# A convolution layer's last stage: rows of e loaded ahead of the output store and the x load, and r3*x+k0 ahead of the copy of x on ScalarE

## The chip, the cores and the metric

The kernel runs on one core of a Trainium2 chip. A core has a matrix engine (TensorE, PE), three elementwise engines (VectorE or DVE, ScalarE or ACT, GpSimd or POOL), and SyncE (SP), which here issues nearly all transfers. Each engine takes its own instructions in order; engines wait for each other and for transfers through semaphores. A transfer is done by DMA engines, which all of SP's transfers share. The metric is the device time of the whole program in microseconds (us), and the figure compared is the median of several runs.

## The reference

Four layers are applied in turn to x of shape 1 x 256 x 256 x 128 (rows, columns, channels), each as `x = x + layer(gn(x))`, with gn a group normalization over the image: an attention layer, two triangle-multiplication layers, and a convolution layer. Only the last one matters here:

```python
t = relu(c1(x))                       # 3x3 convolution of 128 channels to one
y = concatenate([x[:, :1], x[:, 1:] + t[:, :-1]], axis=1)
u = relu(c1(y))
z_main = u + roll(y, 1, axis=1)       # the last two rows are special cases
...
v = relu(c2(z))                       # c2 is a 128x128 product per pixel (centre tap)
p = concatenate([z[:, :, :1], z[:, :, 1:] + v[:, :, :-1]], axis=2)
r = relu(c2(p))
q_main = r + roll(p, 1, axis=2)       # the last two columns are special cases
return q
```

t and u have one channel. So z is the normalized x, moved down one row, plus one number per pixel, which the kernel calls e (u plus the t that belongs there), added to all 128 channels.

## The kernel before

The four layers follow each other; the change lies in the last stage of the last layer (lines 1431 to 1711), which is written out by hand in the order in which each engine gets its instructions. Data stands with the 128 channels on the partitions. The image is cut into 32 groups of 8 rows (`R = 8`, `NR = 32`), each 128 x 2048 floats or 1 MB, and the one-channel images into 16 blocks of 16 rows (`NB = 16`), so two groups make one block. The normalization is folded in: r3 and k0 are a scale and an offset per channel.

For a group s:

- `load9` loads p_x (9 buffers), eight steps ahead.
- `taps`, six steps ahead, multiplies x by the nine taps' weights (PE, p_pp), adds an offset (ACT, p_st) and stores four small pieces to DRAM (sD).
- `load_block` gathers the nine shifted taps back as p_S. `sum_taps` adds them up (DVE, p_acc, L1494) and makes t (p_t, L1496 and L1497); `keep_t` stores t (tD), and `load_t` loads it back one row lower. `image_u` makes u from nine neighbours of t (L1511 to L1515), and `image_e` adds u and the loaded t to e (p_e, L1520) and stores it (eD).
- `load_e` loads the two groups' rows of e of a block as one partition's row each (p_er, 8 KB each), and `spread_e` copies such a row to all 128 partitions on POOL (p_eb, one buffer).
- `start_z` writes r3*x + k0 of a group to PSUM on ACT (p_zp, three or four instructions), and `finish_z` adds p_eb to it on DVE: p_z (L1566).
- `p_half` multiplies p_z by the centre tap (PE, p_pm) and makes p_pb from it (DVE, L1580). `q_half`, one step later, multiplies p_pb and makes p_q (DVE, L1594 and L1597). p_q begins as a copy of x with its offset (ACT, L1672), to which POOL adds p_pb (`residual`, L1586 to L1588).
- `emit`, two steps later, transposes p_q (PE, p_pt), copies it out of PSUM (ACT, p_o) and stores 1 MB of output.

PSUM has two pools: one of two buffers for p_pm, and one of two buffers that p_zp, p_pp and p_pt share in turn. The loop runs over steps s = 0 to 33. In the steady state an even step holds the sum of taps, t and u of a block, an odd step its e and the next gather of taps. SP's order over a pair of steps, from the end of an even one, is: output store, x load, load of t, store of e, four tap stores, two gathers p_S, output store, x load, two loads of e, store of t, four tap stores. A transfer that waits holds up all behind it. x loads end with step 23.

## Time and profile before

| | us |
|---|---|
| runs of the kernel before | 3385.05, 3386.2, 3391.52 (median 3386.2) |
| profiled execution, its run | 3389.84 |
| span in the profile | 3388.1 |
| last stage, from the first x load (2951.2) to the end of the span | 437 |
| PE busy in the whole span | 3085.6 (91%) |
| DVE busy | 2281.1 (67%) |
| ACT busy | 2030.0 (60%) |
| POOL busy | 1666.1 (49%) |

The shares are averages over four layers with different limits. For this change only the last stage counts, and in it the order of time: a row of the profile gives the start and the duration of an instruction, its engine, its line, what it writes and reads, and in brackets how long the engine had been idle before it and what ended that. "SPq" rows are the issue of a transfer, not the transfer itself.

### The profile page before, as it was taken

How to read it: one execution, taken by the hardware profiler on the slowest of the kernel's cores; microseconds unless marked ns; L12 is line 12 of the kernel's file. 1: busy time of each engine (PE TensorE's matmuls, PEld its weight loads, DVE VectorE, ACT ScalarE, POOL GpSimd, SP SyncE). 2: the span in 40 equal slices, each digit the busy share in tenths (PEclk: the TensorE clock that was granted, in tenths of full speed). 3: DMA queues.
4: the chain of work that ended last, by engine and by line, in shares of the span. 5: the costliest groups of instructions: out<-in, count | busy, mean ns of one | idle time of the engine just before them, and what ended most of it. 6: DMA issues, size and time to landing. Idle time of an engine off the chain costs nothing. (4 is left out here: it accounts for less than half of the span.)

```text
span 3388.1 us, 52060 instructions
## 1 busy us (share of the span) xinstructions
PE 3085.6 (91%) x20018; PEld 1636.1 (48%) x20018; DVE 2281.1 (67%) x2612; ACT 2030.0 (60%) x2241; POOL 1666.1 (49%) x908
## 2 busy tenths in 40 slices
PE   5669999999999999967996999999999999748888
PEld 4415555555555555533432444445999333214444
DVE  5627888888888888853555445454555777648787
ACT  3567777777777777734686445443444566636665
POOL 4055777777777777720483000001555344436565
PEclk8889999999999999989897999999999999879999
DMA  9982333333333333369597668676999899736764
GB/s 367 365 310 85 108 121 108 120 108 120 108 120 108 120 108 120 108 270 346 195 409 302 256 257 312 230 258 251 353 349 347 308 334 335 286 115 198 215 191 131
DMA packets 298104, 749.49 MB, mean 221 GB/s; under 512 B 74713, under 2 KB 145323, under 8 KB 248699
## 3 DMA queue, kind: packets, MB, share of 16 engines
q1 hardware_dynamic: 289787, 735.24, 60.6%
q0 software_dynamic: 7776, 9.81, 0.8%
q8 instruction: 160, 2.62, 0.3%
q10 hardware_dynamic: 288, 1.05, 0.1%
q14 instruction: 93, 0.76, 0.1%
HBM read 458.35 MB, written 287.64 MB: 220 GB/s over the span
## 5 line engine op out<-in xcount | busy, mean ns | idle before, releaser
L564 DVE TENSOR_TENSOR p_e<-p_S,triT 128x1024 f32<-128x1024 f32 x512 | 609.4, 1212 | 144.3 <-PE p_S L554 144.3
L574 POOL TENSOR_TENSOR p_es<-p_e 128x1024 f32<-128x1024 f32 x256 | 602.8, 2366 | 124.4 <-issue 65.5
L572 ACT ACTIVATE p_e<-p_e,mbT 128x1024 f32<-128x1024 f32 x512 | 552.0, 1138 | 59.8 <-DVE p_e L564 59.7
L1167 PE MATMUL p_pm<-p_zn,wf 128*128 128x512 f32 x1040 | 449.3, 593 | 2.1 <-ACT p_a L1202 1.9
L539 PE MATMUL p_mm<-p_xn,w 128*128 128x512 f32 x768 | 406.6, 613 | 0.3 <-DVE p_v L534 0.3
L1167 PEld LDWEIGHTS p_pm<-p_zn,wf 128*128 128x128 f32 x1040 | 196.5, 190 | 254.9 <-issue 246.3
L554 PE MATMUL p_S<-p_q,p_k 32*128 32x256 f32 x4096 | 295.7, 401 | 3.3 <-DVE p_e L564 3.3
L554 PEld LDWEIGHTS p_S<-p_q,p_k 32*128 32x128 f32 x4096 | 186.1, 184 | 159.2 <-PE p_mm L530 91.7
L513 POOL TENSOR_TENSOR p_xn<-p_xn,p_rs 128x1024 f32<-128x1024 f32 x63 | 151.2, 2401 | 207.7 <-ACT p_xn L508 131.6
L1852 PE MATMUL tp_z<-p_B,tp_at 128*128 128x256 f32 x1024 | 250.6, 388 | 0.8 <-DMA p_B<-bD 0.5
L1239 POOL DMA_DIRECT2D rs__17906<-rs2D x4 | 2.0, 514 | 506.9 <-DVE p_zn L1160 506.9
L587 PE MATMUL p_o<-p_e,p_v 128*32 128x256 f32 x4096 | 247.6, 382 | 0.0
L1282 POOL TENSOR_TENSOR k<-k,p_sq 128x512 f32<-128x512 f32 x128 | 163.0, 1273 | 156.9 <-ACT p_sq L1280 156.9
L1392 POOL TENSOR_TENSOR p_x<-p_x,p_g 128x2048 f32<-128x2048 f32 x30 | 136.3, 4543 | 160.5 <-DVE p_g L1379 97.2
L1852 PEld LDWEIGHTS tp_z<-p_B,tp_at 128*128 128x128 f32 x1024 | 185.2, 191 | 23.6 <-DVE tp_at L1843 1.6
L1586 POOL TENSOR_TENSOR p_q<-p_q,p_pb 128x2024 f32<-128x2024 f32 x32 | 144.9, 4529 | 70.0 <-DVE p_pb L1580 69.5
L539 PEld LDWEIGHTS p_mm<-p_xn,w 128*128 128x128 f32 x768 | 126.5, 191 | 105.5 <-issue 89.5
L1281 DVE TENSOR_TENSOR k<-tp_z,k 128x512 f32<-128x512 f32 x128 | 88.5, 692 | 127.2 <-ACT p_sq L1280 127.2
L587 PEld LDWEIGHTS p_o<-p_e,p_v 128*32 128x32 f32 x4096 | 120.0, 109 | 109.3 <-ACT p_g L545 41.5
L1278 ACT COPY p_K<-tp_z 128x512 f32<-128x512 f32 x128 | 74.9, 585 | 157.8 <-PE tp_z L1852 157.8
L545 ACT ACTIVATE p_g<-p_mm,bgh 128x512 f32<-128x512 f32 x128 | 87.9, 687 | 131.4 <-PE p_mm L539 131.4
L530 PEld LDWEIGHTS p_mm<-w,p_xn 128*128 128x128 f32 x1024 | 134.4, 191 | 61.1 <-issue 60.6
(377 smaller groups left out, 5945.9 us busy)
## 6 DMA issues: line engine op xcount, KB each, us to landing
p_x<-x2T SPq DMA_DIRECT2D x60, 1024.0 KB
x<-x1T SPq DMA_DIRECT2D x51, 1024.0 KB
p_x<-in_x_dram SPq DMA_DIRECT2D x32, 1024.0 KB
p_x<-xT SPq DMA_DIRECT2D x64, 512.0 KB
x2T<-x SPq DMA_DIRECT2D x32, 1024.0 KB
aD<-p_a SPq DMA_DIRECT2D x32, 1024.0 KB
bD<-p_b SPq DMA_DIRECT2D x32, 1024.0 KB
p_A<-aD SPq DMA_DIRECT2D x32, 1024.0 KB
```

Of the source, the lines that this page charges most:

```text
L513: nc.gpsimd.tensor_tensor(xn, xn, groups[g]["rs"], ALU.mult)
L539: nc.tensor.matmul(pm, lhsT=w, rhs=t["xn"][:, cs_], start=True, stop=True)
L554: nc.tensor.matmul(Ss[h // 2][:, h % 2, u, :], lhsT=t["k"][hp, r * N + u * P : r * N + (u + 1) * P], rhs=t["q"][hp, r * N : (r + 1) * N], ...
L564: nc.vector.tensor_tensor(e[:, :, 2 * p : 2 * p + 2, :].rearrange("p u h n -> p h u n"), Ss[p], triT[:, 2 * p : 2 * p + 2, :, :], ALU.add,)
L572: nc.scalar.activation(e[:, u, :, :], e[:, u, :, :], AF.Exp, bias=mbT[:, u, i : i + 1])
L574: nc.gpsimd.tensor_tensor(es, e[:, 0, :, :], e[:, 1, :, :], ALU.add)
L587: nc.tensor.matmul(t["o"][hp, r % 2, :], lhsT=t["v"][:, r * 2 + u, hp], rhs=e[:, u, h, :], start=(u == 0), stop=(u == 1),)
L1167: nc.tensor.matmul(pm[:, c, :], lhsT=wf2[:, i, :], rhs=zns[s][:, k * CK : (k + 1) * CK], start=True, stop=True)
L1282: nc.gpsimd.tensor_tensor(k2, k2, sq, ALU.add)
L1392: nc.gpsimd.tensor_tensor(xs7[s], xs7[s], gts[s], ALU.add)
L1586: nc.gpsimd.tensor_tensor(q[:, :, 1 : N - 2], q[:, :, 1 : N - 2], pb[:, :, 0 : N - 3], ALU.add)
L1852: nc.tensor.matmul(pz[:, t, :], lhsT=at[:, u, t * P : (t + 1) * P], rhs=Bc[:, u, :], start=(u == 0), stop=(u == 1))
```

## The change

In a step, `start_z` of the next group is called before the copy of x to p_q instead of after it. `load_e`, which an even step called near its beginning (after the x load and after the output store of the step before), is called at the end of the odd step before it, after `load_block` and ahead of `emit`. The same blocks are loaded, and no buffer, shape or operation differs.

```diff
             if s % 2 == 1 and 2 < b < NB:
                 load_t(b)
-            if s % 2 == 0 and 3 < b <= NB:
-                load_e(b - 1)
             if s < NR:
                 pbs[s] = sb.tile([P, R, N], F32, name="p9_pb")
                 nc.scalar.activation(pbs[s][:, :, 0:1], zs[s][:, :, 0:1], AF.Identity, bias=kcol[:, 0:1])
+                if s + 1 < NR:
+                    start_z(s + 1)
                 qs[s] = sb.tile([P, R, N], F32, name="p9_q", bufs=3)
                 nc.scalar.activation(qs[s], xs[s], AF.Identity, bias=kcol[:, 2:3])
-                if s + 1 < NR:
-                    start_z(s + 1)
                 p_half(s, 0)
                 p_half(s, 1)
                 del xs[s]
...
                 taps(xs[s + LEAD], (s + LEAD) * R, 4)
             if s > 1 and s % 2 == 1 and b + 1 < NB:
                 load_block(b + 1)
+            if s > 1 and s % 2 == 1 and b < NB:
+                load_e(b)
             if s > 1:
                 emit(s - 2)
```

## The prediction

> **What bounds the kernel now.** The edit touches only the last layer, so I read the page for its extent (the last 437 us of a 3388.1 us span), then the chain of waits there, then the list of waits, then the order of time through one pair of steps. The steps come in pairs, because a block of 16 rows is two groups of 8. The waits, from 2990 us on (who waited, for whom, us in total, times, longest):

> ```profile
> POOL p_eb L1543 <- DMA p_er<-eD: 58.5, 9, 17.3
> DVE p_z L1566 <- POOL p_eb L1543: 30.3, 10, 4.2
> DVE p_e L1520 <- DMA p_t<-tD: 20.7, 11, 9.8
> DVE p_z L1566 <- ACT p_zp L1551: 0.2, 1, 0.2
> SPq L1611 <- DMA p_x<-x3T: 18.9, 10, 2.8
> ```

> Both row transfers (e and t) are late in every pair, and p_z never waits for ScalarE's p_zp. One pair in order of time (start, duration, engine, line):

> ```profile
> 3197.81 0.32 SPq L1522 DMA_DIRECT2D eD<-p_e  x1
> ...
> 3200.82 1.05 SPq L1474 DMA_DIRECT2D p_S<-sD  x2
> ...
> 3201.97 0.99 SPq L1611 DMA_DIRECT2D out_dram<-p_o  x1
> ...
> 3203.05 3.75 SPq L1449 DMA_DIRECT2D p_x<-x3T  x1
> ...
> 3206.85 1.30 SPq L1535 DMA_DIRECT2D p_er<-eD  x2
> ...
> 3211.80 2.29 POOL L1543 PARTITION_BROADCAST p_eb<-p_er  x1 [6.58 <-ACT p_q L1687]
> 3211.82 0.41 SPq L1611 DMA_DIRECT2D out_dram<-p_o  x1
> ...
> 3214.12 2.36 DVE L1566 TENSOR_TENSOR p_z<-p_zp,p_eb 128x1024 f32<-128x1024 f32 x2 [3.41 <-POOL p_eb L1543]
> ...
> 3220.33 1.03 DVE L1520 TENSOR_TENSOR p_e<-p_u,p_t 128x33 f32<-128x33 f32 x1 [1.22 <-DMA p_t<-tD]
> ...
> 3221.38 0.32 SPq L1522 DMA_DIRECT2D eD<-p_e  x1
> ```

> The e rows are issued 9.04 us after the store of e, behind the tap rows p_S, 1 MB of output and 1 MB of x, and the chain has 4.76 us from issue to landing (3211.61). The broadcast p_eb had been free to start since 3205.2 (end of POOL's p_q), so it is 6.6 us late; p_z then loses 3.41 us. After it POOL runs p_q (3214.18) and the next p_eb (3219.15 to 3221.45), and p_e ends with that: er landing plus 9.8 us. The t rows land some 1.1 us before. From the e store at 3056.92 to that at 3291.81 are ten pairs: 23.49 us a pair. PE has 9.77 us of work a step (3054.88 to 3064.65 between two p_z products, nothing waiting), DVE about 10 us, so a pair could take some 20.

> [...] er has 4.8 to 6.8 us to landing behind those two megabytes, 2.0 us with an empty queue. [...] this pair, after the x loads are over, has a p_eb that is hardly late:

> ```profile
> 3302.28 2.29 POOL L1543 PARTITION_BROADCAST p_eb<-p_er  x1 [3.07 <-DMA p_er<-eD]
> 3302.32 2.28 DVE L1515 TENSOR_SCALAR p_u<-p_u,b 128x33 f32<-128x33 f32 x1
> ...
> 3305.71 5.30 PE L1572 MATMUL p_pm<-p_pb,w2c 128*128 128x512 f32 x8 [2.65 <-DVE p_pb L1580]
> ...
> 3310.93 1.06 PE L1455 MATMUL p_pp<-p_x,w1f 128*32 128x512 f32 x8
> ...
> 3314.87 0.32 ACT L1670 ACTIVATE p_pb<-p_z,kcol 128x8 f32<-128x8 f32 x1
> ```

> L1515 took 2.28 us instead of 0.24 and ends with p_eb. [...] Here 8 products took 5.30 us after 2.65 us of idle, 3.70 elsewhere; gaps of 2.65, 2.87 and 3.29 us were all followed by slow work, gaps up to 1.88 us never, 2.12 partly, 2.35 not.

> **The change, part by part.** Nothing is added or removed; each engine has the same instructions, and the order changes on ACT and SP alone.

> (1) Both e transfers (8 KB each; 0.6 us of issue when nothing backs up) move ahead of one output store and one x load, and ahead of nothing else. They come after p_S, so their wait for the e store's landing (1.44 us) is over. They should land about 0.5 us after p_S: some 7.5 us after the e store instead of 13.8. The output store and x load follow about 1.3 us later in issue, hidden by the p_S transfers still draining (x is loaded two steps before its use). Reaching further: the program gives SP's transfers eight semaphores in turn, so each waits for the one eight places earlier. Before, the odd step's output store waits for the x load (3211.82, the L1611 row above); now it waits for er, and the next x load for an output store long landed. So t is no longer held by that.

> (2) p_zp (2.67 us) goes ahead of the copy of x to p_q (2.00 us) on ACT. p_z didn't wait for p_zp: worth 0 there. The copy is 2.67 us later, and POOL's p_q needs it. In the slow pair above p_pb starts on ACT 3.94 us after p_pp on PE; the copy ended 2.2 us later, at p_pp + 6.15, and now ends at + 8.82. VectorE ends p_pb at + 7.73 (3318.66). So POOL is held 1.0 us (from p_pb's end + 0.17 to + 1.2), in even steps; in odd ones p_pb comes later than the copy.

> (3) What is late next. POOL's p_q to p_eb is 4.97 us (3214.18 to 3219.15). p_eb then starts at p_pp + 8.82 + 0.10 + 4.97 = 13.89, and L1496 (two SBUF inputs) comes at + 7.73 + 6.25 = 13.98: the whole 2.29 us of p_eb fall on VectorE. Before, POOL sat waiting for er there, and L1496 ran free. The cover was er's lateness, and part 1 takes it away.

> The new loop, from the odd step's p_pb on VectorE to the next odd one: first half to PE 1.33, products 3.70, p_pp to ACT's p_pb 3.94, ACT 4.88 (0.21 + 2.67 + 2.00), hand-over 0.10, POOL 4.97, p_eb 2.29, rest of the image work on VectorE 1.64 (3206.61 to 3208.25): 22.85 us. PE meanwhile: p_z products start at p_pp + 2.81, one step of 9.77, products 3.60: idle from p_pp + 16.18 to + 19.15, 2.97 us. Such gaps were slow in 3 of 3; [...] Price 5.30 - 3.70 = 1.60, so 1.28: 24.13 us a pair, against 23.49.

> Sum: the first pair still gains (copy ends 3060.9, p_eb 3065.97 to 3068.26, p_pb 3069.9, then 2.46 + 0.17 + 4.97 + 2.29: e store at 3079.85 for 3080.47), -0.6. Nine pairs, 9 x 0.64 = +5.8. The two pairs without x loads (3291.81 to 3337.91, 46.1): 24.13 + 23.1 (the last has no p_pp, 1.0 less), +1.1. First steps: their p_q waits hide behind DMA. Last steps: PE-bound at 8.8 us each, POOL 7.3, 0. Together +6.3. The profiled span of 3388.1 (its run 3389.84) becomes 3394.4; the median of the runs lies 1.9 under that span, so **3392 us**, 0.17% more: within the 0.2% that a measurement of this kernel can tell from no change.

> Is t in time? tD follows L1496, at the e store + 11.6 (13.2 behind a slow clock); then p_st's four stores (1.4) and the output store, at about + 13.3 (14.9), where it is + 14.0 before; from there to t's landing 8.4 us as before: 21.7 (23.3), or 22.7 if the x load lands 0.4 late and gates it. The pair takes 22.85 (24.45): 0.15 to 1.15 us to spare.

> **Rivals.** *Slower, from the clock.* Every gap drops the clock: 24.45 a pair, 9 x 0.96 - 0.6 + (24.45 + 23.45 - 46.1 = 1.8) = +9.8: 3396. For it: 3 of 3 gaps, and a slow loop has the same 2.97 us gap. Against: [...] 2.35 us was free. It decides above 85% of the gaps; with half of them the sum is about +1.

> *Faster, e's gain kept.* If the copy is not late (ScalarE further ahead than in the pair I took), p_eb starts 1.0 us sooner and blocks L1496 for 1.2 instead of 2.2; the gap shrinks to about 2 us, the clock holds, and t sets the pair at 22.2: 10 x -1.29 - 1.5 = -14: 3372. For it: 30.3 us of p_z's waits and 18.9 of the store's go. Against: ACT's 3.94 us from p_pp holds in every step that I looked at. It decides where POOL's p_q starts within 0.3 us of p_pb.

> *t takes e's place.* If x and output still hold t for 22 to 23 us and p_e follows, pairs stay at 23.5: 3386. It would need p_q to be in time and t late.

> **How the numbers follow.** Loop with part of the gaps slow, within 0.2%: 0.37, and t in e's place 0.06: same 0.43. Clock slow nearly always, or more delay than I count: slower 0.40. Gain kept: faster 0.17. Range 3374 to 3399: from near the fast rival to the slow one plus 3 us for output and x pushed back by er. The likeliest's own is 3385 to 3393.

> **What would show it.** POOL's wait for p_er gone from the steps with x loads, p_z's wait for p_eb near 0, SP's wait of L1611 for p_x gone. L1496 at some 2.4 us instead of 0.26 in most even steps, POOL's p_q released by ACT's p_q instead of p_pb, PE gaps near 3 us with half-speed clock after most. Pairs of 24.1 us. Wrong if L1496 stays short, if p_q follows p_pb at once, or if p_e waits over 2 us for p_t.

## The result and the profile after

| | kernel before | changed kernel |
|---|---|---|
| first comparison, median of the runs | 3391.52 us (13 runs) | 3400.83 us (13 runs) |
| their ratio, 95% interval | | 1.0043 [1.0022, 1.0063] |
| second comparison, median of the runs | 3389.58 us (38 runs) | 3404.12 us (21 runs) |
| their ratio, 95% interval | | 1.0032 [1.0015, 1.0050] |
| profiled execution, its span | 3388.1 us | 3396.0 us, and 3416.9 us in a second one |
| fourth store of e (the prediction's first, 3056.92 before) to the end | 331.2 us | 340.75 us, and 340.97 us in the second one |
| a pair of steps, mean of the ten after that store | 23.49 us | 24.23 us, and 24.24 us in the second one |

The change makes the kernel slower, by 0.3 to 0.4%. (The ratios are not those of the medians, which are 1.0027 and 1.0043; the first is that of the means.) The forecast was 3392 us, and the measured 3400.8 lies 1.8 us above its range. The last two rows say it more sharply than the medians: single runs of either kernel spread over some 30 us, and where the two profiles of the changed kernel show such a spread (21 us), it had all come up by the start of the last layer, 17 us of it in the stage just before, which the change doesn't touch. From the fourth store of e to the end, the two agree within 0.3 us.

The waits of the changed kernel from 2990 us on (who waited, for whom, us in total, times, longest):

```profile
POOL p_q L1586 <- DVE p_z L1566: 73.3, 14, 7.1
...
PE p_pm L1572 <- DVE p_pb L1580: 42.5, 14, 5.3
...
DVE p_e L1520 <- DMA p_t<-tD: 18.7, 9, 9.5
...
POOL p_eb L1543 <- DMA p_er<-eD: 16.9, 1, 16.9
...
POOL p_q L1586 <- ACT p_q L1672: 7.2, 2, 5.4
```

The broadcast's wait for e has gone from 9 times to one (in the layer's first steps). p_z's wait for p_eb (30.3 us before) and the output store's wait for x (18.9 us) are in the list no more. In their place PE waits 42.5 us for VectorE's p_pb, which has to be done before PE can have a PSUM buffer back; it waited 22.7 us for that before. In the first row the profile names p_z as what released POOL's p_q; the pair below shows that the copy of x on ACT ended last.

A pair in order of time (start, duration, engine, line; in brackets the idle time before and what ended it):

```profile
3199.04 0.32 SPq L1522 DMA_DIRECT2D eD<-p_e  x1
...
3202.73 1.99 ACT L1672 ACTIVATE p_q<-p_x,kcol 128x2048 f32<-128x2048 f32 x1
3203.21 1.36 SPq L1535 DMA_DIRECT2D p_er<-eD  x2
...
3204.85 4.52 POOL L1586 TENSOR_TENSOR p_q<-p_q,p_pb 128x2024 f32<-128x2024 f32 x1 [5.74 <-DVE p_z L1566]
...
3209.82 2.22 DVE L1496 SCALAR_TENSOR_TENSOR p_t<-p_acc,b,p_in 128x41 f32<-128x41 f32 x1
...
3209.83 2.29 POOL L1543 PARTITION_BROADCAST p_eb<-p_er  x1
...
3213.68 2.46 DVE L1580 SCALAR_TENSOR_TENSOR p_pb<-p_pm,kcol,p_z 128x1020 f32<-128x1020 f32 x2
...
3215.01 5.34 PE L1572 MATMUL p_pm<-p_pb,w2c 128*128 128x512 f32 x8 [2.93 <-DVE p_pb L1580]
...
3222.71 0.77 DVE L1520 TENSOR_TENSOR p_e<-p_u,p_t 128x33 f32<-128x33 f32 x1 [0.91 <-DMA p_t<-tD]
...
3223.51 0.32 SPq L1522 DMA_DIRECT2D eD<-p_e  x1
```

Read from the top. The e rows are issued 4.17 us after the store of e, where it was 9.04, and the first lands 2.82 us after its issue, where it took 4.76 (1 MB of output and 1 MB of x ahead of it). p_pb ended at 3203.64 and the copy of x at 3204.72: POOL's p_q starts right after the copy. So p_eb falls on the same moment as L1496 on VectorE, which takes 2.22 us instead of 0.26 and ends with p_eb (at 3212.04 and 3212.12). p_pb is late, PE stands for 2.93 us, and the next eight products take 5.34 us instead of 3.70. That repeats: L1496 takes 2.08 to 2.23 us in every pair from 3064 us on. The trace also records the clock granted to PE, here 1.0 or 0.5 of full speed. The gap of the first pair, as long as the others (2.94 us at 3069.5), was followed by full speed; from the gap at 3092.1 on each has a stretch of half clock, 11 of them between 3092.0 and 3337.8, and two of these, at 3139.8 and 3262.7, last 6.83 us instead of 3.41. The first pair took 22.76 us, the second 22.81 (its p_e waits 1.7 us for t, so that the slow products show only in the next). The eight after it took 24.59 us on average; the two with a long stretch took 25.81 and 25.60.

The table by stretches shows the clock: us from the span's start, length, busy time of PE, PE's weight loads, DVE, ACT and POOL with the number of instructions, granted clock, DMA share, GB/s. First the kernel before, then the changed one:

```profile
3060.00:3300.00 240.00, 209.65 (x831) 100.01 (x831) 194.14 (x247) 153.62 (x185) 148.13 (x83) 0.99 0.69 203
```

```profile
3060.00:3300.00 240.00, 211.32 (x792) 99.92 (x792) 200.65 (x238) 147.22 (x177) 142.45 (x80) 0.92 0.67 198
```

PE is busier in the changed kernel and shows 39 matmuls fewer in the same 240 us: 0.92 of the clock instead of 0.99.

### The profile page after: what moved, and what is told of

Its sections match the earlier page's. It is cut to its first block, busy times and chain, and to the rows that moved or that the text cites. A ratio compares the mean times of both kernels' runs of the same rounds, so it can differ in the third digit from the quotient of the medians.

```text
span 3396.0 us, 52049 instructions
## 1 busy us (share of the span) xinstructions
PE 3096.8 (91%) x20018; PEld 1640.9 (48%) x20018; DVE 2297.5 (68%) x2612; ACT 2029.9 (60%) x2241; POOL 1666.8 (49%) x908
## 3 DMA queue, kind: packets, MB, share of 16 engines
q10 hardware_dynamic: 288, 1.05, 0.1%
## 5 line engine op out<-in xcount | busy, mean ns | idle before, releaser
L1572 PE MATMUL p_pm<-p_pb,w2c 128*128 128x512 f32 x256 | 139.8, 697 | 42.5 <-DVE p_pb L1580 42.5
```

Source lines behind the costliest of these rows:

```text
L1572: nc.tensor.matmul(pm[:, 2 * c : 2 * c + 2, :], lhsT=w2c, rhs=src[:, r : r + 2, :], start=True, stop=True)
```

## The experiments

Two measures are used throughout: "the layer" below is the time from the fourth store of e to the end in the profiled execution (331.2 us before, 340.75 changed), and "a pair" is the mean of the ten pairs after that store. Ratios are to the kernel before, with a 95% interval.

**Each half of the change alone.** First the move of `load_e`, without that of `start_z`:

```diff
-            if s % 2 == 0 and 3 < b <= NB:
-                load_e(b - 1)
...
+            if s > 1 and s % 2 == 1 and b < NB:
+                load_e(b)
             if s > 1:
                 emit(s - 2)
```

> The kernel before with the move of load_e alone; start_z stays behind the copy of x. My theory (late copy -> p_eb meets L1496 whole -> PE gap of 2.9 us -> half clock): with the copy in time POOL's p_q follows p_pb, p_eb runs from p_pp + 12.87 to + 15.16 and holds L1496 for 1.2 us instead of 2.2; the PE gap shrinks to about 2 us, the clock holds in most pairs, and the pair is 21.8 by the loop or 22.2 by t: 12 to 16 us under the kernel before. Rival (the early e alone costs: any meeting of p_eb and L1496, or the output store and x load behind e, slows the pair): pairs of 23.5 us or more, no gain or a loss.

Measured: 3380.77 us against 3392.22, 0.9958 [0.9941, 0.9974]; the layer 317.1 us (14.1 less), a pair 22.59 us. Three rows of its order of time, from two pairs:

```profile
3162.41 5.40 PE L1572 MATMUL p_pm<-p_pb,w2c 128*128 128x512 f32 x8 [1.90 <-DVE p_pb L1580]
...
3181.75 0.93 DVE L1496 SCALAR_TENSOR_TENSOR p_t<-p_acc,b,p_in 128x41 f32<-128x41 f32 x1
...
3185.65 3.70 PE L1572 MATMUL p_pm<-p_pb,w2c 128*128 128x512 f32 x8 [1.75 <-DVE p_pb L1580]
```

L1496 is held for about 1 us (0.86 to 1.25 in all) instead of 2.2, the PE gap is 1.3 to 2.1 us instead of 2.9, and only three of them dropped the clock. VectorE's wait for t has grown to 24.1 us from 3060 to 3300 us (9.2 in the changed kernel); that t limits the pair here is shown further below. This is what the rival *Faster, e's gain kept* in the prediction describes, and its sum of -14 us. A meeting of p_eb with L1496 that holds it for 1 us, and not for 2, does not make the kernel slower.

Then the move of `start_z` alone:

```diff
+                if s + 1 < NR:
+                    start_z(s + 1)
                 qs[s] = sb.tile([P, R, N], F32, name="p9_q", bufs=3)
                 nc.scalar.activation(qs[s], xs[s], AF.Identity, bias=kcol[:, 2:3])
-                if s + 1 < NR:
-                    start_z(s + 1)
```

> The kernel before with the move of start_z alone; load_e stays behind the output store and the x load. My theory: er lands 6.6 us later than POOL could use it, so a copy of x that is 2.67 us later (p_q held 1.0 us) is hidden, L1496 stays at 0.26 us, and the time is that of before within 3 us. Rival (the late copy is what costs in the changed kernel, by itself): 5 to 10 us slower, with POOL's p_q held by the copy and long PE gaps.

Measured: 3391.16 us, 0.9992 [0.9978, 1.0006]; the layer 329.3 us, a pair 23.53. Its waits between 3060 and 3300 us, and two rows of a pair:

```profile
POOL p_eb L1543 <- DMA p_er<-eD: 34.5, 6, 6.7
...
DVE p_z L1566 <- POOL p_eb L1543: 30.3, 10, 4.2
...
POOL p_q L1586 <- ACT p_q L1674: 29.8, 9, 4.6
```

```profile
3201.12 4.53 POOL L1586 TENSOR_TENSOR p_q<-p_q,p_pb 128x2024 f32<-128x2024 f32 x1 [3.23 <-ACT p_q L1674]
...
3206.38 0.26 DVE L1496 SCALAR_TENSOR_TENSOR p_t<-p_acc,b,p_in 128x41 f32<-128x41 f32 x1
```

POOL's p_q now follows the copy of x, so the copy is late here too; but e is later still, p_eb comes after L1496, and nothing is lost. The two halves alone give -14.1 and -1.9 us in the layer, together +9.6: all of the loss is in their meeting.

**The clock.** In the changed kernel the second half of the p_z product is done twice, into the same PSUM tile, in odd steps (1.8 us of PE work in the 2.9 us gap; 16 steps, 29 us of work added in all):

```diff
         def p_half(s, h):
             rows_ = slice(h * H, (h + 1) * H)
             pm = product9(zs[s], h)
+            if h == 1 and s % 2 == 1:
+                for c in range(2):
+                    r = h * H + 2 * c
+                    nc.tensor.matmul(
+                        pm[:, 2 * c : 2 * c + 2, :], lhsT=w2c, rhs=zs[s][:, r : r + 2, :], start=True, stop=True
+                    )
```

> The changed kernel with the second half of the p_z product done twice, into the same PSUM tile, in each odd step: 1.8 us of PE work put into the 2.8 to 2.9 us gap, nothing else moved. If the clock is what makes pairs of 24.2 to 25.8 us: no half clock in these gaps, the loop's own 22.85 us a pair, 11 pairs x 1.6 to 1.8 us = 17 to 20 us under the changed kernel, some 3380 us or 7 to 10 us under the kernel before. If the lock and POOL's chain alone make the pair and the clock is hidden: no change against the changed kernel, 0.4% above before; if PE is the bound: slower by up to 29 us.

Measured: 3392.62 us, 0.9993 [0.9975, 1.0010]; the layer 325.2 us, which is 15.5 under the changed kernel, a pair 22.67. The same stretch of the table, and the gap in one pair:

```profile
3060.00:3300.00 240.00, 227.49 (x885) 107.78 (x884) 214.23 (x257) 158.18 (x189) 152.44 (x85) 1.00 0.70 208
```

```profile
3179.91 1.88 PE L1583 MATMUL p_pm<-p_z,w2c 128*128 128x512 f32 x4
...
3182.89 3.70 PE L1572 MATMUL p_pm<-p_pb,w2c 128*128 128x512 f32 x8 [1.10 <-DVE p_pb L1586]
```

More work on the busiest engine made the layer shorter. The gap is 1.10 us, no stretch of half clock is left in the ten pairs (one follows at 3320.3, and one over the last 6 us, as at the end of every kernel here), L1496 still takes 2.06 to 2.25 us in all pairs but one (1.56), and the pair is the loop's own. So of the changed kernel's pair of 24.2 the clock is 1.6 us. The expectation had 17 to 20 us under the changed kernel, a little more than the 15.5 found. The time of the whole program can't tell this kernel from the kernel before: by the layer it would be 6 us, or 0.18%, shorter, which lies within the interval.

The same addition on the kernel with `load_e` moved alone:

> The kernel with load_e moved alone, with the second half of the p_z product done twice in odd steps: the 1.9 us gaps are nearly filled. If the clock costs that kernel only where a gap dropped it (3 of 10 pairs x 1.6 us): no half clock, 4 to 6 us under it, pairs of 22 us limited by t. If filled PE time pushes t or q: no gain.

Measured: 3375.86 us, 0.9960 [0.9945, 0.9975]; the layer 313.2 us (3.9 under that kernel), a pair 21.82, clock 1.00. By the trace it is near what was expected (4 to 6 us, no half clock); the ratios of the two (0.9958 and 0.9960) cannot tell them apart.

**The changed kernel once more**, unchanged:

> The changed kernel again, unchanged, beside the others on one chip. If the slow clock in every pair is all there is, its last layer is the loop of the first profile: pairs of 24.2 to 24.6 us, 10 us over the kernel before (ratio near 1.003); if the 14.6 us of the first comparison hold (ratio near 1.0043), part of the loss is still without a cause.

Measured: 3404.12 us against 3389.58, 1.0032 [1.0015, 1.0050]; the layer 340.97 us, with the same pairs to within 0.1 us and the same two long stretches of half clock. The loss in the layer, 9.6 to 9.8 us, is 0.28 to 0.29% and lies within both intervals.

**The meeting of p_eb and L1496.** It can be taken away without leaving work out: p_eb is put behind an operation on POOL that waits for VectorE's work on u. The first attempt moved the scalar operation on u to POOL:

```diff
-            nc.vector.tensor_scalar(k["u"], k["u"], b1, 0.0, ALU.add, ALU.max)
+            (nc.gpsimd if b > 2 else nc.vector).tensor_scalar(k["u"], k["u"], b1, 0.0, ALU.add, ALU.max)
...
                 residual(s)
-                spread_e(s + 2)
+                late = s > 1 and s % 2 == 0 and b < NB
+                if not late:
+                    spread_e(s + 2)
...
                     image_u(b)
+                    spread_e(s + 2)
```

> The changed kernel with the last operation on u (L1515, scalar add and max) done on POOL, and the even step's p_eb behind it, so that p_eb starts after VectorE's image work (p_t, p_prod, p_u) instead of beside it; same instructions otherwise. If the meeting of p_eb and L1496 opens the PE gap: L1496 back at 0.26 us in even steps, the gap near 1 us, no half clock there, and the pair 22.85 - 2.0 = 20.9 us by the loop, or some 22 by t: 15 to 25 us under the kernel before. If the late copy of x is what counts: the gap and the pairs of 24 us stay.

Measured: 3665.4 us, 1.0797 [1.0765, 1.0828]. POOL's rows in one pair:

```profile
3307.44 2.30 POOL L1543 PARTITION_BROADCAST p_eb<-p_er  x1 [8.14 <-issue]
3316.87 4.49 POOL L1586 TENSOR_TENSOR p_q<-p_q,p_pb 128x2024 f32<-128x2024 f32 x1 [7.12 <-ACT p_o L1610]
...
3327.72 2.30 POOL L1543 PARTITION_BROADCAST p_eb<-p_er  x1 [5.99 <-issue]
3337.03 4.62 POOL L1586 TENSOR_TENSOR p_q<-p_q,p_pb 128x2024 f32<-128x2024 f32 x1 [7.01 <-issue]
```

POOL stands idle for 6 to 9 us ahead of nearly every broadcast and every p_q, and a pair takes 43.2 us. L1496 is 0.26 us, but with such gaps the run says nothing on the changed kernel's clock. The trace has what precedes them, instructions that no other run has in the last stage (number; shortest, median and longest in ns; first and last start):

```profile
L1543 POOLq MODIFY_POOL_CONFIG  x56: 1/1/24, 3040.3 to 3617.3; - x56
L1586 POOLq MODIFY_POOL_CONFIG  x56: 129/129/129, 3050.1 to 3625.1; - x56
```

Two of them stand ahead of each of 28 broadcasts and 28 p_q, and from the second one to the work behind it 5.5 to 8.9 us pass. So the idle time came with the scalar operation in POOL's work, at each change between the broadcast and the additions, and each time behind these instructions; what POOL does in these 6 to 9 us no row shows.

The second attempt keeps to kinds that POOL had there already: the two-operand addition on u goes to POOL, p_eb behind it, and the scalar operation stays on VectorE and moves to `image_e`, a step later.

```diff
         def image_u(b):
...
-            nc.vector.tensor_tensor(k["u"], k["u"], k["acc"][:, 0:BW], ALU.add)
-            nc.vector.tensor_scalar(k["u"], k["u"], b1, 0.0, ALU.add, ALU.max)
+            (nc.gpsimd if b > 2 else nc.vector).tensor_tensor(k["u"], k["u"], k["acc"][:, 0:BW], ALU.add)
...
         def image_e(b):
             k = blocks.pop(b)
             e = sb.tile([P, BW], F32, name="p9_e")
+            nc.vector.tensor_scalar(k["u"], k["u"], b1, 0.0, ALU.add, ALU.max)
```

with `spread_e` moved as above.

> The changed kernel with the even step's addition on u (L1514, two operands) done on POOL, p_eb behind it there, and the scalar add and max on u moved from image_u to the start of image_e, a step later: the same instructions otherwise, and on POOL only kinds that stand there already. If the meeting of p_eb and L1496 opens the PE gap: L1496 at 0.26 us, the gap at 1 us or less, no half clock there, the loop at 22.85 - 2.0 - 0.4 = 20.5 us, t (whose store follows L1496 2 us earlier) at some 21 to 22: 15 to 25 us under the kernel before. If the late copy of x is what counts, the gap and the pairs of 24 us stay.

Measured: 3376.47 us, 0.9961 [0.9941, 0.9980]; the layer 310.7 us, 30 under the changed kernel and 20.5 under the kernel before, a pair 22.12. One pair:

```profile
3188.25 0.26 DVE L1496 SCALAR_TENSOR_TENSOR p_t<-p_acc,b,p_in 128x41 f32<-128x41 f32 x1
...
3189.81 0.26 POOL L1514 TENSOR_TENSOR p_u<-p_u,p_acc 128x33 f32<-128x33 f32 x1 [3.19 <-DVE p_u L1513]
3190.04 2.29 POOL L1543 PARTITION_BROADCAST p_eb<-p_er  x1
3190.97 3.70 PE L1572 MATMUL p_pm<-p_pb,w2c 128*128 128x512 f32 x8 [0.53 <-DVE p_pb L1580]
```

L1496 is short in every pair and the gap that it opened is 0.53 us here and no longer in the others, although p_zp still goes ahead of the copy of x. Two stretches of half clock are left, where none was expected; they follow gaps of 2.32 and 2.54 us in the other step of a pair, not at the place of L1496. So the late copy costs through this meeting alone, which the next run confirms. But the pair is 22.1 us and not 20.5: VectorE now waits 30.7 us for t in ten pairs. The same on the kernel with `load_e` moved alone:

> The same rearrangement of u and p_eb on the kernel that moves load_e alone. If the remaining 1.1 us of L1496 and the 1.9 us PE gaps are what hold that kernel's pair at 22.6: pairs of 21 to 22 us, limited by t. If t already sets the pair there (VectorE waited 1.5 us for it), nothing more than the earlier tD store, 1 us a pair, is gained.

Measured: 3373.85 us, 0.9951 [0.9929, 0.9973]; the layer 311.7 us, a pair 22.16. With the copy early or late it is the same pair. And t holds the pair already with `load_e` moved alone: VectorE's wait for it is 31.1 us here, and the earlier store of t brings 0.4 us a pair, where up to 1 was expected.

**What sets the pair then.** In the odd step the load of t goes ahead of the x load:

```diff
-            load9(s + 8)
             b = s // 2 + 2
             if s % 2 == 1 and 2 < b < NB:
                 load_t(b)
+            load9(s + 8)
```

> As the last one, and the odd step's load of t ahead of that step's x load. If t behind 1 MB of x sets the pair: VectorE's wait for p_t before p_e goes, the e store comes 1 to 2 us earlier, and pairs fall to PE's 20 to 21 us: 20 to 30 us under the kernel before. If the tD store or the semaphore that t shares with earlier transfers sets it: no change from the run without this move.

Measured: 3357.68 us, 0.9904 [0.9878, 0.9931]; the layer 294.0 us, a pair 20.36. VectorE's wait for t between 3060 and 3300 us, first in the kernel without this move, then with it:

```profile
DVE p_e L1520 <- DMA p_t<-tD: 31.1, 10, 4.1
```

```profile
DVE p_e L1520 <- DMA p_t<-tD: 2.2, 4, 1.0
```

No PE gap over 0.8 us and no half clock is left up to 3280 us, and PE is busy for 215.6 of the 220 us from 3060 us on: PE is the bound. The same with p_zp ahead of the copy, as in the changed kernel:

> The last rearrangement (e early, u and p_eb deferred, t ahead of the x load) with p_zp ahead of the copy of x as in the changed kernel. If the order of p_zp and the copy matters only through the meeting of p_eb with L1496: PE-bound pairs of 20.2 to 20.5 us as without it, within 3 us of that run. If the later copy has a price of its own (POOL's p_q 1.0 us later, p_eb and p_z after it): pairs of 21 us or more, 8 us or more above it.

Measured: 3350.49 us, 0.9869 [0.9842, 0.9896]; the layer 294.5 us, a pair 20.29. The order of p_zp and the copy, which cost the changed kernel some 24 us against `load_e` moved alone (340.75 to 317.1), is worth nothing here. Both versions are faster than the kernel before, by 1.0 and 1.3%, and so than the changed one; they were run six and four times, on different chips, and their intervals overlap.

## Why the prediction was wrong

*Right: the order of events.* The forecast put p_eb at p_pp + 13.89, L1496 at + 13.98, and PE's idle time from + 16.18 to + 19.15. In the pair above (p_pp at 3195.91) they are at + 13.92, + 13.91, and + 16.17 to + 19.10. POOL's p_q is held 1.0 us by the copy, as said. The loop without the clock, 22.85 us by the sum, is 22.76 in the first pair and 22.67 with the gap filled.

*Right: the parts by themselves.* Part 2 "worth 0" while e is late: the run with it alone shows -1.9 us in the layer and no difference in the times. Part 1's gain of 14 us, in the rival that keeps it: 14.1. Only their meeting costs, as part 3 said. The rival *t takes e's place* didn't come about here, but t is what limits the pair as soon as the meeting is gone.

*Right in effect, not in size.* t was to have 0.15 to 1.15 us to spare. VectorE does wait for it, 0.91 us in the pair shown and 1.7 at most, 9.2 us in 8 of the ten pairs; that is under the 2 us that the prediction names as a sign of being wrong, and it doesn't set the pair: with the gap filled the wait is 19.2 us and the pair 22.67. The prediction shows L1515 held beside p_eb (2.28 us instead of 0.24) and says of L1496 that it has two SBUF inputs. L1515 has one tensor, p_u, and a value per partition, b, so it is no example of two tensors. L1496, with the two tensors p_acc and p_in, and L1520, with p_u and p_t, show the same in the profiles before and after: from 3040 us on, the 15 of L1496 and the 25 of L1520 that ran beside a p_eb ended 0.08 to 0.09 us before it, L1496 after 1.04 to 2.23 us (0.26 alone), L1520 after 0.33 to 1.81 (0.20 at the shortest). p_eb took 2.29 to 2.30 us each time. L1580 and L1594, which read a PSUM tile, kept their 1.27 to 1.28 us beside it, and L1494, with one tensor, its 1.34 to 1.36. Why L1515 was held, in its one meeting there, isn't shown.

*Wrong: the share of slow gaps.* This is the step that failed in the account of the change. The sum's 1.28 us a pair are 0.8 of the price of 1.60; the 0.8 was the author's estimate, and it was too low. From the second pair on every gap was slow, and two drops lasted twice as long: 24.59 us a pair where the sum had 24.13. The two pairs without x loads were slow as well, 48.7 us where the sum had 47.2. Together the layer is 9.6 us longer (9.8 in the second profile) where the forecast had 6.3. That is the rival *Slower, from the clock*, worked out at +9.8 us and 24.45 a pair. I gave it and other delays 0.40 and the partly slow loop 0.37.

| window | PE idle in it, us | windows | the next one at half clock |
|---|---|---|---|
| at full clock | 1.88 to 2.87 | 27 | 27 |
| at full clock | 0 to 1.83 | 718 | 0 |
| at half clock | 0.67 to 1.53 | 5 | 5 |
| at half clock | 0 to 0.56 | 27 | 0 |

In these windows the border is some 1.85 us of idle time inside one, and, to stay slow, some 0.6. It is a border of this stage: over their whole spans the profiles before and after have 74 drops to half clock, 11 of them behind a window with 0.99 to 1.83 us of idle time, and six windows with 1.85 to 1.96 us had none behind them; 13 windows at half clock with under 0.6 us were followed by another. In the stage it sorts all the gaps: the 1.88, 1.90 and 2.09 us gaps with `load_e` moved alone lay each within one window, the other one of 1.88 and that of 1.89 were divided by a border, and the forecast's "gaps up to 1.88 us never" was a matter of place. By this border a gap of 2.94 us is free only if a border divides it into two parts under 1.85, that is, if the gap ends 1.09 to 1.85 us after a border: (1.85 - 1.09) / 3.41 = 0.22 of all places. For a place drawn at random, then, some 0.78 of the gaps would be slow, near the 0.8 of the sum; that is an estimate from the table.

But the place is not random in a loop. Against the window's border nearest to it, the first eleven gaps of the changed kernel end at + 1.3 us (the first pair, free), then + 0.1, + 0.6, + 0.7, - 0.9, - 0.4, + 0.1, + 0.4, + 0.7, - 1.0, - 0.4: a pair of 24.2 to 24.5 is a little over seven windows (23.9), so the place moves on by some 0.4 us a pair; at + 0.7 the half-clock window holds over 0.6 us of the gap, the drop lasts a second window, and the longer pair (25.6 to 25.8, seven and a half windows) throws the place back to about - 1. It never comes to the free places from + 1.1 on. The second profile of the changed kernel shows the same sequence. The borders of 1.85 and 0.6 are read from the traces, and only the runs with the gap filled test them by an edit (1.1 to 1.2 us of idle time, no drop); no run moved the window.

*Wrong too, and more in us: the base.* The forecast started from the 3386.2 us of three runs. The same kernel has 3391.5 us in 13 runs, these three among them, and 3389.6 to 3392.2 in later series. So of the 8.8 us between forecast and result some 5 are the base, and 3.3 the clock's share. The range of 3374 to 3399 had room for the slow rival on the low base, and none for a base that three runs had put 5 us too low.

## What to carry to other kernels

Two edits that each cost nothing or gain can lose together: the early e was cover for the late copy, so before removing a wait, ask what has been running beside something slow only because of that wait. The 2 us that L1496 lost beside p_eb reached PE as a gap of 2.8 to 2.9 us, and the half clock behind it added 1.6 us a pair (24.2 against 22.67 with the gap filled). Here a PE gap of 2 to 3 us was free or slow by how much of it fell into one window, and in a loop that lasts nearly whole windows that can be slow in almost every turn, as here (11 of 12). And a single median of three runs was 5 us off for a change of 10. The change as meant had its gain behind two small moves (p_eb behind the addition on u, t ahead of x), which made the pair 20.3 us instead of 24.2.

## What was not expected of the hardware

- Filling a PE gap with 1.8 us of repeated products, 29 us of work in all, made the last layer 15.5 us shorter.
- The clock's border from 3062 to 3300 us: up to 1.83 us of idle time in a 3.41 us window at full clock was never followed by half clock, 1.88 us and more always was, in 745 windows of eleven traces; at half clock, 0.67 us and more was followed by another such window (5 of 5). Over the whole span it was not as sharp: 11 of 74 drops in the profiles before and after came below it. In the two pairs of the changed kernel with such a second window the products ran slow throughout (6.74 us in one, against 5.34 with one window and 3.70 at full clock).
- One 33-element scalar operation a pair on POOL, 0.45 us by itself, cost some 19 us a pair by the 6 to 9 us of idle time, each after a MODIFY_POOL_CONFIG, ahead of POOL's other work; a two-operand addition of the same size (0.26 us) left none.
